# One-hot forms on VectorE in the edge loops of a two-layer graph network, and a fourth row buffer in its attention layer

## Chip, cores and metric

The kernel runs on one core of a Trainium2 chip. The metric is the device time of one execution in microseconds. The kernel before took 15652.3 us, the median of three runs (15645.26 to 15654.0).

## What is computed

A graph has N = 12500 nodes of D = 128 features and E = 400000 edges, sorted by their target `dst`. Two blocks follow each other, each added to the residual stream. The first is a relational graph convolution (RGCN) in two layers over R = 10 edge types; the second is graph attention (GAT) with 4 heads of 32 channels. The reference, cut to what matters:

```python
edge_type = argmax(edge_attr[:, 16:26], axis=1)            # msg[:, 16:-16]

def rgcn(x, w_rel, root, bias):
    seg = dst * R + edge_type
    mean = segment_sum(x[src], seg) / maximum(segment_sum(1, seg), 1)   # per target and type
    return einsum('nrd,rdo->no', mean.reshape(N, R, D), w_rel) + x @ root + bias

h = relu(layernorm(x))
x = x + rgcn(relu(rgcn(h, w_rel1, root1, b1)), w_rel2, root2, b2)

h = relu(layernorm(x))
xl, xr = h @ W_l, h @ W_r                                  # 4 heads x 32
score = einsum('ehc,hc->eh', leaky_relu(xr[dst] + xl[src], 0.2), att)
ex = exp(score - segment_max(score, dst)[dst])
x = x + segment_sum(ex / segment_sum(ex, dst)[dst] * xl[src], dst) + bias
```

## The kernel before

**Tables and rows.** Each layer first makes a table in HBM with all rows that an edge can ask for. `transform` fills `t1_d` with the ten products of a node's features with the ten relation matrices, one row of 128 floats for each node and type. An edge then needs one row of the table, number `src * 10 + type`, and it contributes that row times 1/count to its target. Layer 1's own loop writes the table of layer 2 (`t2_d`) as its results appear, and layer 2's loop writes the table of GAT (`xl_d`, 132 floats a row, and `xr_d`).

**Groups.** The edges are cut into G = 125 groups of 3200, as 128 partitions by J = 25 columns. Since edges are sorted by target, a group touches fewer than 128 consecutive targets. `gather` (L326 to L332) issues 25 indirect DMAs for a group on GpSimd's queue (L329), each of which brings one row to each of the 128 partitions, into a buffer `xs` of the pool; the pools hold three such buffers in all three layers. The same loop therefore runs three times over 125 groups: layer 1, layer 2, GAT.

**Sums on TensorE.** To add rows by target, VectorE makes for each of the 25 columns a one-hot matrix `s` of 128 edges by 128 targets, times the edge's weight, from a row of the numbers 0 to 127 (`iota`, in SBUF), the target column `dst_f` and the weight column `w` (L351). TensorE multiplies it with the gathered rows and accumulates in PSUM over the columns (L353). Six buffers of `s` let VectorE run ahead. `carry` (L356 to L363) adds what the group before left for a shared target.

**Layer 1** (`load`, `weights`, `work`). `load` finds each edge's type on VectorE: the maximum of ten attributes (L384), a compare and a multiply with the constants `rel_m` of -10 to -1 (L386, L387), a minimum (L389), plus 10 (L390), and from it the row numbers `idx` (L391) that the gathers wait for. It then builds one-hots of type (`rh`, L395) and target (`sb`, L397, 3200 elements a partition in bf16) and counts edges by target and type on TensorE (`pcn`, L401). `weights` for the group before adds the counts that a target has in the neighbouring groups (`pcf`, L409 to L416), takes the counts back to the edges with the one-hot `st` (`by_node`, L334 to L340: the targets of a group as a row, loaded onto all partitions as `db`, compared with the partition's own number `pcol`), and takes the reciprocal (L424 to L428). `work`, two groups behind, makes the sums and from them the next table.

**Layer 2** has only the gathers, the sums with the weights that layer 1 left, a normalization (`normed_T`, whose last step is `hn`, L123) and the projections for GAT, split into three bf16 parts (L506 to L514).

**GAT** (`scores`, `rows`). `scores` gathers the group's rows, brings the targets' `xr` to the edges with `st` on TensorE (L564 to L568), applies ReLU on ScalarE (L571), and multiplies with `att` and reduces on VectorE (L572, L574), in seven chunks of up to four columns; then it takes running maxima over each target. `rows` for the group before needs a value from the group after (`after[-1]`), takes exponentials, multiplies rows by them (`xw`, L626), makes one-hots (`s`, L630), and sums on TensorE (L634). `xw` is the last reader of a row buffer.

**The order of the work.** The framework orders each engine's instructions when the program is built: the loops are written group by group, and the built order interleaves neighbouring groups on each engine by its own planned times. An engine then runs its instructions strictly in that order, so one that waits holds what stands behind it. GpSimd has nothing but gathers in these loops; SP's queue carries the plain loads and stores.

Of the kernel before, what the change touches and what calls it, by code (L numbers as in the profile page):

```python
# [9 lines left out]
F32 = mybir.dt.float32  # L10
I32 = mybir.dt.int32
BF16 = mybir.dt.bfloat16
# [14 lines left out]
def kernel(  # L27
# [84 lines left out]
    def normed_T(pool, psum, xt):  # L112

        st = pool.tile([P, nc.vector.BN_STATS_DIM], F32, name="st")
        nc.vector.bn_stats(st, xt)
        mv = pool.tile([P, nc.vector.BN_AGGR_DIM], F32, name="mv")
        nc.vector.bn_aggr(mv, st)
        sd = pool.tile([P, 1], F32, name="sd")
        nc.scalar.activation(sd, mv[:, 1:2], AF.Sqrt, bias=epsc)
        rs = pool.tile([P, 1], F32, name="rs")  # L120
        nc.vector.reciprocal(rs, sd)
        hn = pool.tile([P, D], F32, name="hn")
        nc.vector.tensor_scalar(hn, xt, mv[:, 0:1], rs, op0=OP.subtract, op1=OP.mult)  # L123
        return relu_T(pool, psum, hn)
# [133 lines left out]
    def relation_consts(pool):  # L258
        rel_m = pool.tile([P, J, R], F32, name="rel_m")
        nc.gpsimd.iota(rel_m, pattern=[[0, J], [1, R]], base=-R, channel_multiplier=0,  # L260
                       allow_small_or_imprecise_dtypes=True)
        return rel_m


    def sorted_edges():
# [3 lines left out]
        with tc.tile_pool(name="sd", bufs=1, space=DRAM) as sd, tc.tile_pool(name="sk", bufs=1) as sk:  # L269
# [11 lines left out]
            nc.vector.tensor_copy(iotab, iota)  # L281
            identb = sk.tile([P, P], BF16, name="identb")
# [51 lines left out]
            def by_node(pool, dpool, g):  # L334
# [4 lines left out]
                nc.vector.tensor_scalar(st.rearrange("q j p -> q (j p)"), db, pcol, None, op0=OP.is_equal)  # L339
# [3 lines left out]
            with tc.tile_pool(name="mid", bufs=1) as mid:  # L343
# [3 lines left out]
                def sums(sp, psum, g, xs):  # L347
                    ps = psum.tile([P, D], F32, name="ps")
                    for j in range(J):
                        s = sp.tile([P, P], F32, name="s")  # L350
                        nc.vector.tensor_scalar(s, iota, dst_f[:, g, j:j + 1], w[:, g, j:j + 1],  # L351
# [13 lines left out]
                def layer1():  # L365
                    with tc.tile_pool(name="fk", bufs=1) as kp, tc.tile_pool(name="fx", bufs=3) as xp, \
# [4 lines left out]
                        rel_m = relation_consts(kp)  # L371
                        iotar = kp.tile([P, J, R], F32, name="iotar")
                        nc.vector.tensor_scalar_add(iotar, rel_m, float(R))
# [5 lines left out]
                        def load(g):  # L379
# [26 lines left out]
                        def weights(g, rh, cn, before, after):  # L406

                            pcf = p1.tile([P, R], F32, name="pcf")
# [18 lines left out]
                            nc.vector.tensor_scalar_max(cs, cs, 1.0)  # L427
                            nc.vector.reciprocal(w[:, g, :], cs)  # L428

                        def work(g, xs, before):  # L430
# [5 lines left out]
                            ps = sums(sp, p2, g, xs)  # L436
# [28 lines left out]
                def layer2():  # L465
                    with tc.tile_pool(name="hk", bufs=1) as kp, tc.tile_pool(name="hx", bufs=3) as xp, \
                            tc.tile_pool(name="hs", bufs=6) as sp, tc.tile_pool(name="hc", bufs=4) as cp, \
                            tc.tile_pool(name="hp", bufs=2, space=PSUM) as p2:
                        bob = bcast_row(kp, bias, "bob")
# [18 lines left out]
                        def work(g, xs, before):  # L488
# [3 lines left out]
                            ps = sums(sp, p2, g, xs)  # L492
# [36 lines left out]
            with tc.tile_pool(name="gk", bufs=1) as kp, tc.tile_pool(name="gx", bufs=3) as xp, \  # L529
# [71 lines left out]
                def rows(g, now, after, before):  # L601
# [41 lines left out]
                    nc.vector.tensor_scalar_add(rd, sm[:, :, C:], 1e-16)  # L643
# [431 lines left out]
```

## Time and profile before

The profiled execution took 15668.01 us; the span of its instructions is 15666.2 us.

| Stage (us from the start) | PE busy | VectorE busy | GpSimd busy | TensorE clock granted |
|---|---|---|---|---|
| layer 1, 479 to 5605 | 2194.95 | 1845.23 | 3340.91 | 0.63 |
| layer 2, 5650 to 10159 | 1824.76 | 1174.33 | 2969.91 | 0.57 |
| GAT, 10197 to 15608 | 2975.87 | 2523.45 | 3434.30 | 0.71 |
| whole span | 7415.8 | 5907.1 | 9747.0 | 0.649 |

The stages are told by the gathers: each begins with the first and ends with the last of its 3125. How to read a group's line: source line, engine, operation, what it writes and reads, how many; then busy time, mean time of one in ns, the idle time of the engine just before these instructions, and who ended most of that idle time. "issue" is time that no traced wait explains, and "remote" a wait whose end no traced instruction explains. A timeline's line has the start and the length in us first, and the idle time before it, with its releaser, in brackets at its end. [...]

### The profile page before, as it was taken

To read this page: it belongs to the slowest core of one execution; us is meant where nothing else is said; L and a number is where in the kernel's file an instruction comes from. 1 tells how busy PE (TensorE), PEld (TensorE's weight loads), DVE (VectorE), ACT (ScalarE), POOL (GpSimd) and SP (SyncE) were. 2 spreads that over 40 slices of the span, in tenths; PEclk is the share of its full clock that TensorE was granted. 3 is DMA by queue.
4 is the path that set the end of the run, shared out by engine and by line. 5 is a ranking of instruction groups with operands and counts; after the bars stand their busy time and mean duration, and the time that the engine had idled before them with its cause. 6 is when DMAs were issued, how large, how long until landed. Compare 5 with 4: busy or idle time off the path is not lost.

```text
span 15666.2 us, 128693 instructions
## 1 busy us (share of the span) xinstructions
PE 7415.8 (47%) x39724; PEld 5085.2 (32%) x39724; DVE 5907.1 (38%) x16500; ACT 1459.9 (9%) x4672; POOL 9747.0 (62%) x9384
## 2 busy tenths in 40 slices
PE   7344444444344433444344444445555555555555
PEld 2223333322232322333233333333333433333333
DVE  5333333333333322222222222244444544444444
ACT  2000000000000000000000000011111111111111
POOL 0566666666666656666666666656666666666665
PEclk9666666666666655555555555567766777767777
DMA  6322323323332211111111111122222222222221
GB/s 202 111 92 91 96 92 96 96 90 95 94 96 92 91 59 53 54 54 54 53 54 55 55 54 54 52 68 63 66 62 64 65 62 66 62 66 65 62 64 51
DMA packets 626065, 1164.38 MB, mean 74 GB/s; under 512 B 196480, under 2 KB 398830, under 8 KB 625390
## 3 DMA queue, kind: packets, MB, share of 16 engines
q0 software_dynamic: 300000, 621.40, 14.7%
q1 hardware_dynamic: 279544, 456.64, 8.8%
q10 hardware_dynamic: 45846, 78.02, 1.4%
q8 instruction: 341, 5.59, 0.1%
q14 instruction: 334, 2.74, 0.1%
HBM read 949.89 MB, written 205.49 MB: 74 GB/s over the span
## 4 chain that ended last, share of the span: by engine, by line
another core or an unknown queue 34%; POOL 19%; PE 19%; issue 14%; DVE 9%; DMA 4%; ACT 1%; ACTq 0%; SPq 0%; DVEq 0%; POOLq 0%
POOL xs L329 19%; PE ps L353 9%; DVE s L351 4%; PE pz L564 2%; PE pt L445 2%; DMA xs<-xl_d,src_i 2%; PE po L634 2%; DVE xw L626 1%; PE pz L568 1%; PE ps L150 1%; DMA xs<-t_d,idx 1%; DMA xt<-in_x_dram 1%; DVE sb L397 1%; PE ptr L128 1%
## 5 line engine op out<-in xcount | busy, mean ns | idle before, releaser
L329 POOL DMA_INDIRECT xs<-t_d,idx x6250 | 6310.8, 1010 | 3815.1 <-issue 2597.7
L353 PE MATMUL ps<-xs,s 128*128 128x128 f32 x12500 | 3119.0, 392 | 4870.9 <-issue 2743.4
L329 POOL DMA_INDIRECT xs<-xl_d,src_i x3125 | 3434.3, 1099 | 2014.9 <-DVE xw L626 1046.8
L353 PEld LDWEIGHTS ps<-xs,s 128*128 128x128 f32 x12500 | 2411.9, 267 | 5713.7 <-issue 3732.0
L351 DVE TENSOR_SCALAR s<-iota,dst_f,w 128x128 f32<-128x128 f32 x6250 | 2019.8, 359 | 5559.5 <-remote 3662.8
L564 PE MATMUL pz<-xs,ident 128*128 128x512 f32 x1750 | 1297.5, 834 | 2097.2 <-DMA xs<-xl_d,src_i 1219.8
L564 PEld LDWEIGHTS pz<-xs,ident 128*128 128x128 f32 x1750 | 355.6, 254 | 2229.6 <-issue 1559.7
L568 PEld LDWEIGHTS <-st 128*128 128x128 bf16 x9375 | 840.9, 126 | 622.7 <-issue 558.1
L572 DVE TENSOR_TENSOR lr<-lr,att 128x512 f32<-128x512 f32 x875 | 533.5, 624 | 1259.3 <-ACT lr L571 855.0
L568 PE MATMUL pz<-xr,st 128*128 128x128 bf16 x9375 | 956.5, 269 | 65.2 <-DVE st L339 49.9
L634 PE MATMUL po<-xw,s 128*128 128x132 f32 x6250 | 848.8, 297 | 76.5 <-DVE xw L626 41.2
L634 PEld LDWEIGHTS po<-xw,s 128*128 128x128 f32 x6250 | 815.9, 208 | 122.6 <-issue 64.4
L362 ACT COPY sm<-ps 128x128 f32<-128x128 f32 x250 | 66.3, 265 | 7564.5 <-PE ps L359 4030.8
L571 ACT ACTIVATE lr<-pz 128x512 f32<-128x512 f32 x875 | 476.8, 551 | 2776.4 <-remote 1425.1
L630 DVE TENSOR_TENSOR s<-iotab,dst_b 128x640 f32<-128x640 bf16 x625 | 506.6, 814 | 420.8 <-PE po L634 354.9
L626 DVE TENSOR_TENSOR xw<-xs,xw 128x640 f32<-128x640 f32 x625 | 484.0, 819 | 156.0 <-ACT xw L625 122.3
L574 DVE TENSOR_REDUCE sc<-lr 128x16 f32<-128x512 f32 x875 | 531.3, 620 | 1.0
L445 PE MATMUL pt<-wall,hT 128*128 128x512 f32 x750 | 504.3, 827 | 57.0 <-ACT hT L130 41.0
L397 DVE TENSOR_TENSOR sb<-iotab,dst_b 128x3200 bf16<-128x3200 bf16 x125 | 434.9, 3479 | 0.9 <-PE pcn L401 0.9
L424 DVE TENSOR_TENSOR cw<-pc,rh 128x250 f32<-128x250 f32 x125 | 51.9, 415 | 726.7 <-remote 619.8
L150 PE MATMUL ps<-wall,hT 128*128 128x512 f32 (+1 forms) x588 | 300.9, 647 | 29.1 <-DVE ts L155 21.4
L445 PEld LDWEIGHTS pt<-wall,hT 128*128 128x128 f32 x750 | 183.4, 268 | 305.1 <-issue 175.8
(187 smaller groups left out, 4532.6 us busy)
## 6 DMA issues: line engine op xcount, KB each, us to landing
db<-drow_d SPq DMA_DIRECT2D x250, 800.0 KB
xs<-t_d,idx POOLq DMA_INDIRECT x6250
t_d<-ts SPq DMA_DIRECT2D x125, 640.0 KB
m<-in_edge_attr_dram SPq DMA_DIRECT2D x125, 525.0 KB
t_d<-ts ACTq DMA_DIRECT2D x98, 640.0 KB
xs<-xl_d,src_i POOLq DMA_INDIRECT x3125
ac<-acc_d SPq DMA_DIRECT2D x250, 64.0 KB
xr_d<-xp SPq DMA_DIRECT2D x125, 96.0 KB
```

The source lines that it names most:

```text
L329: nc.gpsimd.indirect_dma_start(out=xs[:, j, :], out_offset=None, in_=table, in_offset=bass.IndirectOffsetOnAxis(ap=ids[:, j:j + 1], axis=0))
L351: nc.vector.tensor_scalar(s, iota, dst_f[:, g, j:j + 1], w[:, g, j:j + 1], op0=OP.is_equal, op1=OP.mult)
L353: nc.tensor.matmul(ps, s, xs[:, j, :], start=(j == 0), stop=(j == J - 1), skip_group_check=True)
L397: nc.vector.tensor_tensor(sb, iotab[:, None, :].to_broadcast([P, J, P]), dst_b[:, g, :, None].to_broadcast([P, J, P]), op=OP.is_equal)
L445: nc.tensor.matmul(pt[:, :n], hT, wall[:, c:c + n], start=True, stop=True)
L564: nc.tensor.matmul(pz[:, :n, :], ident, xs[:, j0:j0 + n, :D], start=True, stop=False, skip_group_check=True)
L568: nc.tensor.matmul(pz[:, j, :], st[:, j0 + j, :], xr[:, k, :], start=False, stop=(k == 2), skip_group_check=True)
L572: nc.vector.tensor_mul(lr[:, :n, :], lr[:, :n, :], att8[:, None, :].to_broadcast([P, n, P]))
L574: nc.vector.tensor_reduce(sc[:, :, j0:j0 + n].rearrange("p h j -> p j h"), lr[:, :n, :].rearrange("p j (h c) -> p j h c", h=H), AX.X, OP.add)
L626: nc.vector.tensor_mul(xw[:, :, :, :C], xs[:, j0:j0 + JW, :D].rearrange("p j (h c) -> p j h c", h=H), xw[:, :, :, C:].to_broadcast([P, JW, ...
L630: nc.vector.tensor_tensor(s, iotab[:, None, :].to_broadcast([P, JW, P]), dst_b[:, g, j0:j0 + JW, None].to_broadcast([P, JW, P]), op=OP.is_ ...
L634: nc.tensor.matmul(po, s[:, j, :], xw[:, j].rearrange("p h a -> p (h a)"), start=(j0 + j == 0), stop=(j0 + j == J - 1), skip_group_check=True)
```

## The change

In the edge loops, instructions of VectorE are written in other forms, and one pool gets a buffer more:

- The row of numbers is copied once in each of layers 1 and 2 to a PSUM tile `iotap`, and the 25 one-hots of a group (`sums`) read it from there.
- `st` (`by_node`, in layer 1 and GAT) is a comparison of two tensors, the second the bf16 column `pcolb` repeated along the row, where it was a comparison with a scalar column. `er` likewise.
- `hn` reads the reciprocal as a repeated tensor, in a form with three operands.
- In layer 1 the type is found as the minimum of `not_equal * 10 + number`, which needs no constants `rel_m` and no addition afterwards; `max(count, 1)` before the reciprocal is dropped, since an edge's own count is at least 1. The PSUM tile `pcf` takes the name `pcn`, and so shares the single buffer of the tile of that name[...].
- GAT's denominators are read from the PSUM tile `po`, not from its copy `sm`.
- GAT's pool of row buffers (`gx`) has four in place of three.

```diff
-        nc.vector.tensor_scalar(hn, xt, mv[:, 0:1], rs, op0=OP.subtract, op1=OP.mult)
+        nc.vector.scalar_tensor_tensor(hn, xt, mv[:, 0:1], rs.to_broadcast([P, D]), op0=OP.subtract, op1=OP.mult)
...
+            pcolb = sk.tile([P, 1], BF16, name="pcolb")
+            nc.vector.tensor_copy(pcolb, pcol)
...
-                nc.vector.tensor_scalar(st.rearrange("q j p -> q (j p)"), db, pcol, None, op0=OP.is_equal)
+                nc.vector.tensor_tensor(st.rearrange("q j p -> q (j p)"), db,
+                                        pcolb.to_broadcast([P, J * P]), op=OP.is_equal)
...
+                def row_in_psum(psum):
+                    t = psum.tile([P, P], F32, name="iotap")
+                    nc.vector.tensor_copy(t, iota)
+                    return t
...
-                        nc.vector.tensor_scalar(s, iota, dst_f[:, g, j:j + 1], w[:, g, j:j + 1],
+                        nc.vector.tensor_scalar(s, iotap, dst_f[:, g, j:j + 1], w[:, g, j:j + 1],
                                                 op0=OP.is_equal, op1=OP.mult)
...
-                        rel_m = relation_consts(kp)
+                        iotap = row_in_psum(p1)
                         iotar = kp.tile([P, J, R], F32, name="iotar")
-                        nc.vector.tensor_scalar_add(iotar, rel_m, float(R))
+                        nc.gpsimd.iota(iotar, pattern=[[0, J], [1, R]], base=0, channel_multiplier=0,
+                                       allow_small_or_imprecise_dtypes=True)
...
-                            eq = wp.tile([P, J, R], F32, name="eq")
-                            nc.vector.tensor_tensor(eq, z, mx[:, :, None].to_broadcast([P, J, R]), op=OP.is_equal)
-                            nc.vector.tensor_mul(eq, eq, rel_m)
+                            lt = wp.tile([P, J, R], F32, name="lt")
+                            nc.vector.tensor_tensor(lt, z, mx[:, :, None].to_broadcast([P, J, R]), op=OP.not_equal)
+                            nc.vector.scalar_tensor_tensor(lt, lt, float(R), iotar, op0=OP.mult, op1=OP.add)
                             rel = wp.tile([P, J], F32, name="rel")
-                            nc.vector.tensor_reduce(rel, eq, AX.X, OP.min)
-                            nc.vector.tensor_scalar_add(rel, rel, float(R))
+                            nc.vector.tensor_reduce(rel, lt, AX.X, OP.min)
...
-                            pcf = p1.tile([P, R], F32, name="pcf")
+                            pcf = p1.tile([P, R], F32, name="pcn")
...
-                                nc.vector.tensor_scalar(er, iota[0:1, :], eb[0:1, g:g + 1], None, op0=OP.is_equal)
+                                nc.vector.tensor_tensor(er, iota[0:1, :], eb[0:1, g:g + 1].to_broadcast([1, P]),
+                                                        op=OP.is_equal)
...
-                            nc.vector.tensor_scalar_max(cs, cs, 1.0)
...
+                        iotap = row_in_psum(p1)
                         bob = bcast_row(kp, bias, "bob")
...
-            with tc.tile_pool(name="gk", bufs=1) as kp, tc.tile_pool(name="gx", bufs=3) as xp, \
+            with tc.tile_pool(name="gk", bufs=1) as kp, tc.tile_pool(name="gx", bufs=4) as xp, \
...
-                    nc.vector.tensor_scalar_add(rd, sm[:, :, C:], 1e-16)
+                    nc.vector.tensor_scalar_add(rd, po.rearrange("p (h a) -> p h a", h=H)[:, :, C:], 1e-16)
```

More of the change, by code (lines that the diff above doesn't have):

```diff
@@ L256, in analyse @@
             nc.vector.tensor_copy(eb, pb[:, 1, :])
[L258 to L262, printed above, removed]
     def sorted_edges():
@@ L345, in sorted_edges, with sums @@
                 w = mid.tile([P, G, J], F32, name="w")
-                def sums(sp, psum, g, xs):
+                def row_in_psum(psum):
+                    t = psum.tile([P, P], F32, name="iotap")
+                    nc.vector.tensor_copy(t, iota)
+                    return t
+                def sums(sp, psum, iotap, g, xs):
                     ps = psum.tile([P, D], F32, name="ps")
@@ L435, in work @@
                             nc.sync.dma_start(xb, xb_d[ds(b, P), :])
-                            ps = sums(sp, p2, g, xs)
+                            ps = sums(sp, p2, iotap, g, xs)
                             sm = carry(cp, ps, g, before, D)
@@ L467, in layer2 @@
                             tc.tile_pool(name="hs", bufs=6) as sp, tc.tile_pool(name="hc", bufs=4) as cp, \
+                            tc.tile_pool(name="hp1", bufs=1, space=PSUM) as p1, \
                             tc.tile_pool(name="hp", bufs=2, space=PSUM) as p2:
+                        iotap = row_in_psum(p1)
                         bob = bcast_row(kp, bias, "bob")
@@ L491, in work @@
                             nc.sync.dma_start(ac, acc2_d[g])
-                            ps = sums(sp, p2, g, xs)
+                            ps = sums(sp, p2, iotap, g, xs)
                             sm = carry(cp, ps, g, before, D)
```

## The prediction

> **What bounds the kernel now.** I read the page first, for the busy engine and its groups; then the GpSimd groups of each stage alone; then timelines of GpSimd and VectorE in one iteration of layer 2 and of layer 1; then who waits for whom in the GAT stage.
>
> ```profile
> POOL 0566666666666656666666666656666666666665
> ...
> L329 POOL DMA_INDIRECT xs<-t_d,idx x6250 | 6310.8, 1010 | 3815.1 <-issue 2597.7
> ...
> L329 POOL DMA_INDIRECT xs<-xl_d,src_i x3125 | 3434.3, 1099 | 2014.9 <-DVE xw L626 1046.8
> ...
> L351 DVE TENSOR_SCALAR s<-iota,dst_f,w 128x128 f32<-128x128 f32 x6250 | 2019.8, 359 | 5559.5 <-remote 3662.8
> ```
>
> GpSimd does nothing but row gathers and is the busiest engine from the first edge group to the last. VectorE's one-hots (L351) stand behind 5559 us of idle time, most of it "remote": no traced instruction ended the wait.
>
> The groups of GpSimd in layer 1 (479 to 5605 us), layer 2 (5650 to 10159) and GAT (10197 to 15608):
>
> ```profile
> L329 POOL DMA_INDIRECT xs<-t_d,idx x3125 | 3340.9, 1069 | 2231.4 <-issue 1709.1 <-DVE idx L391 447.0 <-PE ps L353 29.3
> ...
> L329 POOL DMA_INDIRECT xs<-t_d,idx x3125 | 2969.9, 950 | 1583.7 <-issue 888.6 <-PE ps L353 320.5 <-remote 267.7
> ...
> L329 POOL DMA_INDIRECT xs<-xl_d,src_i x3125 | 3434.3, 1099 | 2014.9 <-DVE xw L626 1046.8 <-issue 908.7 <-DVE rest L512 39.1
> ```
>
> Busy plus idle is 5572, 4554 and 5449 us. The pace at which gathers follow each other undisturbed is in the timelines below: 0.945 us and 0.30 us of issue. For 3125 gathers that is 2953 + 938 = 3891 us, in each stage. The rest splits in two. Busy time over 2953 is gathers held up: 388, 17 and 481 us. Idle time over 938, less each stage's first wait (447, 46, 39 us), is GpSimd waiting for a buffer or an index: 846, 600 and 1038 us. These 2484 us of gaps and 886 us of hold-ups are what a change can win.
>
> Layer 2, GpSimd and then VectorE:
>
> ```profile
> 7532.03 0.94 POOL L329 DMA_INDIRECT xs<-t_d,idx  x1 [0.30 <-issue]
> 7533.27 0.97 POOL L329 DMA_INDIRECT xs<-t_d,idx  x1 [0.30 <-issue]
> 7539.16 0.97 POOL L329 DMA_INDIRECT xs<-t_d,idx  x1 [4.91 <-PE ps L359]
> ...
> 7501.80 1.88 DVE L351 TENSOR_SCALAR s<-iota,dst_f,w 128x128 f32<-128x128 f32 x7 [1.06 <-PE ps L353]
> ...
> 7524.65 0.35 DVE L351 TENSOR_SCALAR s<-iota,dst_f,w 128x128 f32<-128x128 f32 x1 [3.21 <-remote]
> 7528.19 0.35 DVE L351 TENSOR_SCALAR s<-iota,dst_f,w 128x128 f32<-128x128 f32 x1 [3.19 <-issue]
> 7533.08 0.35 DVE L351 TENSOR_SCALAR s<-iota,dst_f,w 128x128 f32<-128x128 f32 x1 [4.54 <-remote]
> 7537.29 0.35 DVE L351 TENSOR_SCALAR s<-iota,dst_f,w 128x128 f32<-128x128 f32 x1 [3.86 <-remote]
> 7538.71 1.63 DVE L351 TENSOR_SCALAR s<-iota,dst_f,w 128x128 f32<-128x128 f32 x6 [1.07 <-PE ps L353]
> ```
>
> While gathers run, one-hots come 3.5 to 4.9 us apart; in GpSimd's pause (7534.2 to 7539.2) they come 0.27 us apart. Rows landed long before, so data isn't missing. The loop feeds on itself: gathers starve the one-hots of an older group, that group keeps its buffer, and GpSimd pauses about 5 us in every group until VectorE has caught up.
>
> Layer 1 shows the opposite hold: VectorE on GpSimd.
>
> ```profile
> 2895.21 3.48 DVE L397 TENSOR_TENSOR sb<-iotab,dst_b 128x3200 bf16<-128x3200 bf16 x1
> 2895.60 3.91 POOL L329 DMA_INDIRECT xs<-t_d,idx  x1 [0.30 <-issue]
> 2899.81 0.94 POOL L329 DMA_INDIRECT xs<-t_d,idx  x1 [0.30 <-issue]
> ```
>
> One gather takes 3.91 us because it meets the 3.48 us one-hot sb, a two-input form: 2.96 us lost. Layer 1's whole hold-up, 388 us over 125 groups, is 3.1 us a group. Where within its 1.25 us a gather meets sb varies, so the loss does too; counting each lengthened gather to the VectorE instruction that overlaps it most, 2.7 us a group are sb's, the rest L339's and L351's. In GAT:
>
> ```profile
> POOL xs L329 <- DVE xw L626: 1046.8, 97, 40.8
> ...
> PE pz L564 <- DMA xs<-xl_d,src_i: 1219.8, 362, 19.4
> ```
>
> GpSimd waits for the release of a row buffer by xw, while TensorE waits for rows: neither is saturated, and three buffers tie them together.
>
> [...] L424, PSUM input, 250 elements, 415 ns against 412 for L386 from SBUF[...]. [...] sb, so built, takes 3479 ns for 3200 elements (1.04 ns each and some 150)[...].
>
> **The change part by part.**
>
> *The one-hots of layers 1 and 2 (6250 of L351) read PSUM.* Price of one: 415 ns less 122 x 1.04 = 288 ns, 359 now. [...] nothing should stop them during gathers. TensorE then sets their pace: where nothing held them, twelve matmuls (six edge columns of two passes) took 2.93 us on TensorE's timeline, so 25 columns take 12.2 us. A group's work of 12 to 15 us fits under 31 us of gathers, with two buffers' slack. Layer 2's 600 us of gaps go; I leave 10. Its two-input forms (L495, L497, L512 twice, now L123) take 0.29 us each and cost little: the present hold-up is 17 us, and I keep 10. Layer 2: 46 + 3891 + 10 + 10 = 3957, against 4554: -597. In layer 1 the next index chain (L384 to L391) stands on VectorE behind these one-hots, so its gaps have the same source. In the built order the chain still follows the older group's one-hots; without waits VectorE needs about 25 x 0.5 us, 7 us for sb and st, and some 5 us on TensorE, 25 us in all, before the next index is ready. I leave 40 us of 846.
>
> *st (L339), 250 times, becomes two-input.* Now 1064 ns; then as sb, 3479 ns. On VectorE that adds 2.4 us a group, which lies beside gathers: VectorE is busy 1845 of 5126 us in layer 1 and 2523 of 5411 in GAT. On GpSimd it doesn't hide: as sb it should hold gathers 2.7 us a group. Bounds: what st costs already (by the same count 0.2 us a group in layer 1 and 1.1 in GAT, 134 us), and 3.4, its whole length. I take 2.7, 340 us a stage.
>
> Layer 1: 447 + 3891 + sb 340 + st 340 + others 25 + gaps 40 = 5083, against 5572: -489.
>
> *The fourth row buffer in GAT.* Gather group g+3 must now wait for xw of group g; in the built order that stands behind up to four score chunks of group g+2, hence pauses of 12 us after a group ends. With four buffers the waiting group is g+4: one whole group's gathers, 37 us, lie between. The gaps go if compute keeps up. TensorE waits for rows 1220/125 = 9.8 us of its 43.4 us a group, so it needs about 33.6, and st's 2.4 makes 36; GpSimd needs 31.1 and hold-ups. These are now 481 us, of them 134 by the present st; the other 347 arise while GpSimd works, 80% of the time, so 434 when it always does; with 340 of st, 774 us, or 37.3 us a group in all. The two are close: I leave 100 us of gaps. GAT: 39 + 3891 + 774 + 100 = 4804, against 5449: -645. The whole gain here hangs on compute needing under 37 us.
>
> *One answer each, zero:* the dropped add and max of layer 1 (0.18 and 0.23 us) and the merged PSUM tile (pcf waits for the scalar copy of pcn, under 0.5 us twice a group; TensorE is busy 2195 of 5126 us): slack of the gathers covers them, and without it they would cost at most 125 us. hn in three-operand form, about 0.29 for 0.35 us, beside gathers; in the first 390 us it is 98 times -0.06. The denominators from PSUM; the iota on GpSimd ahead of the first index; pcolb and row copies, once.
>
> **Sum.** -597 - 489 - 645 = -1731 us. The profiled execution took 15668.0 (its span 15666.2 and 1.8 around it), 15.7 above the median 15652.3. 15668 - 1731 = 13937, less 16: about 13920.
>
> **Rivals.**
> - *GAT is bound by compute.* For it: 36 against 37 us is close, and the order interleaves two groups with ScalarE waits (pz for lr, 514 us). Against it: TensorE waits for rows a fifth of the time. At 41.5 us a group GAT ends 3 us x 125 = 390 higher: 14310.
> - *Two-input holds are cheaper than sb's.* If st costs what it does now and gaps vanish: 315 + 206 + 150 lower, 13250; at half of that, 13580. For it: some st fall into pauses or next to sb; against: gathers never pause then.
> - *The new one-hot still contends, and st's hold comes on top (slower).* For it: the two scalar columns still come from SBUF, and no row shows such a form. Then layers 1 and 2 keep their gaps, and st adds 2.4 us to VectorE's catch-up in a pause plus 2.5 to a run in layer 1 (613 us). GAT gains nothing if its chain, lengthened by st's 2.4 us, is the bound (300 us). 15652 + 913 is 16570. It decides when gaps shrink by less than 2.5 us a group. Against: two-input forms start within gathers freely.
>
> **How the numbers follow.** Forecast 0.64, compute-bound GAT 0.18, cheap holds 0.12, slower 0.06. Range 13550 to 14450: cheap holds at half, up to compute-bound GAT with 140 us of gaps left in layer 1. A difference under 0.2% can't be told from none here. Faster 0.93, same 0.01, slower 0.06.
>
> **What would show it.** One-hots in layer 2 about 0.5 us apart during gathers, their "remote" idle gone; GpSimd's idle in layer 2 near 1000 us; gathers of 3 to 4 us beside st in layer 1 and GAT, their busy time near 3660 and 3730 us; no wait for xw over 1 us in most GAT groups. Wrong if one-hots still come 3 us apart, if st doesn't lengthen a gather, or if GpSimd still waits for xw.

## The result, and the profile after

The kernel after takes 17071.66 us (median of 4 runs, 17048.29 to 17082.26) where the kernel before, on the same chip, takes 15648.78 (4 runs, 15638.42 to 15654.0): 1.0908 times as long, 95% interval 1.0889 to 1.0927. The profiled execution's span is 17060.9 us. The page of the kernel after; its lines stand a few further down: gathers L325, one-hots L354, st L335, sb L400, cw L428.

```profile
POOL 0454444444444444666666666666677677766665
...
L325 POOL DMA_INDIRECT xs<-t_d,idx x6250 | 5928.8, 949 | 5413.9 <-issue 4109.3
...
L325 POOL DMA_INDIRECT xs<-xl_d,src_i x3125 | 3862.1, 1236 | 1737.8 <-issue 933.7
...
L354 DVE TENSOR_SCALAR s<-iotap,dst_f,w 128x128 f32<-128x128 f32 x6250 | 2262.6, 401 | 5072.2 <-remote 3579.7
```

In layers 1 and 2 the gathers themselves became shorter (5928.8 us for 6310.8), but GpSimd's idle time grew from 3815.1 to 5413.9. One one-hot takes 401 ns, not less than 359, and still stands behind 5072 us of idle time, "remote" as before. The groups of GpSimd in layer 1 (479 to 6704 us), layer 2 (6748 to 11375) and GAT (11419 to 16975):

```profile
L325 POOL DMA_INDIRECT xs<-t_d,idx x3125 | 2971.2, 951 | 3699.6 <-issue 3206.6 <-DVE idx L394 446.7 <-PE ps L356 38.9
...
L325 POOL DMA_INDIRECT xs<-t_d,idx x3125 | 2957.5, 946 | 1714.2 <-issue 902.7 <-PE ps L356 743.9 <-PE ptr L486 45.2
...
L325 POOL DMA_INDIRECT xs<-xl_d,src_i x3125 | 3862.1, 1236 | 1737.8 <-issue 933.7 <-DVE xw L631 756.1 <-ACT xr L319 44.3
```

Counted from the gathers' starts and ends in the two traces, means per group of 25 gathers in us ("hold-up" is what gathers last over 0.945 us each; the run contains it):

| Stage | before: run, hold-up, pause, period | after: run, hold-up, pause, period | whole stage, before to after, us |
|---|---|---|---|
| layer 1 | 34.06, 3.14, 7.00, 41.08 | 31.11, 0.16, 18.83, 49.94 | 5125 to 6224 |
| layer 2 | 31.08, 0.17, 5.02, 36.10 | 30.98, 0.05, 6.08, 37.06 | 4507 to 4627 |
| GAT | 34.79, 3.88, 8.56, 43.38 | 38.21, 7.28, 6.28, 44.55 | 5410 to 5556 |

So the stages changed by +1099, +119 and +146 us, where the forecast had -489, -597 and -645. The loss lies in layer 1: its pauses grew by 11.83 us a group, while its hold-ups shrank by 2.98. A timeline of layer 1 after, in order of time:

```profile
2502.45 0.78 PE L404 MATMUL pcn<-rh,sb 128*128 128x10 bf16 x25
2502.80 0.95 POOL L325 DMA_INDIRECT xs<-t_d,idx  x1 [19.14 <-issue]
...
2504.95 0.17 ACT L406 CAST cn<-pcn 128x10 bf16<-128x10 f32 x1 [3.93 <-remote]
...
2506.07 0.85 PE L426 MATMUL pc<-cf,st 128*128 128x10 bf16 x25
...
2521.42 0.42 DVE L428 TENSOR_TENSOR cw<-pc,rh 128x250 f32<-128x250 f32 x1 [17.42 <-remote]
...
2532.80 0.94 POOL L325 DMA_INDIRECT xs<-t_d,idx  x1 [0.30 <-issue]
...
2538.31 4.27 DVE L354 TENSOR_SCALAR s<-iotap,dst_f,w 128x128 f32<-128x128 f32 x13 [2.42 <-remote]
2542.82 3.48 DVE L400 TENSOR_TENSOR sb<-iotab,dst_b 128x3200 bf16<-128x3200 bf16 x1
2547.28 3.47 DVE L335 TENSOR_TENSOR st<-db,pcolb 128x3200 bf16<-128x3200 bf16 x1
2552.42 0.95 POOL L325 DMA_INDIRECT xs<-t_d,idx  x1 [18.67 <-issue]
```

Two things are to be seen. cw (the counts of each edge, the step before its weight) needs only pc and rh; rh was done at 2502.4 and TensorE ended pc at 2506.9, yet cw starts at 2521.4, and the group's last 19 one-hots stand behind it on VectorE. And in GpSimd's pause (2533.7 to 2552.4) thirteen one-hots, sb and st stand one after the other ahead of the next idx: 4.6 us of waiting, 4.3 of one-hots, 3.5 and 3.5, and 2.9 of small steps. In the kernel before, the sb that stood behind idx was the next group's, and in 111 of 125 groups it started while a gather ran.

In layer 2 after, the one-hots from PSUM come as far apart as those from SBUF did:

```profile
9030.98 0.94 POOL L325 DMA_INDIRECT xs<-t_d,idx  x1 [0.30 <-issue]
9031.42 0.41 DVE L354 TENSOR_SCALAR s<-iotap,dst_f,w 128x128 f32<-128x128 f32 x1 [3.10 <-remote]
...
9034.98 0.41 DVE L354 TENSOR_SCALAR s<-iotap,dst_f,w 128x128 f32<-128x128 f32 x1 [3.15 <-remote]
...
9039.22 0.41 DVE L354 TENSOR_SCALAR s<-iotap,dst_f,w 128x128 f32<-128x128 f32 x1 [3.83 <-remote]
```

That speaks against the forecast of one-hots about 0.5 us apart. What ends these waits is in the trace's semaphore events, its records of the engines' signals to each other: a one-hot waits for TensorE's signal that the matmul six columns earlier has read its buffer. Of layer 2's one-hots with over 1 us of idle before them, 84% (before) and 90% (after) start within 60 ns of a TensorE signal, the median 26 ns after it. The other direction is prompt, as in the kernel before, where TensorE follows each one-hot here within 0.06 us:

```profile
7524.65 0.35 DVE L351 TENSOR_SCALAR s<-iota,dst_f,w 128x128 f32<-128x128 f32 x1 [3.21 <-remote]
7525.05 0.79 PE L353 MATMUL ps<-xs,s 128*128 128x128 f32 x2 [2.76 <-DVE s L351]
...
7528.19 0.35 DVE L351 TENSOR_SCALAR s<-iota,dst_f,w 128x128 f32<-128x128 f32 x1 [3.19 <-issue]
7528.60 0.79 PE L353 MATMUL ps<-xs,s 128*128 128x128 f32 x2 [2.75 <-issue]
```

Counted over layer 2 of before, from the fourth gather of a run on: the 877 matmuls with over 0.5 us of idle before them start a median 0.06 us after their one-hot's end, while the 982 one-hots with over 1 us of idle start a median 7.9 us after the end, a modelled one, of the matmul six columns earlier. VectorE was ready; TensorE's signal was late.

### The profile page after: what moved, and what is told of

Its sections match the earlier page's. It is cut to its first block, busy times and chain, and to the rows that moved or that the text cites. A ratio compares the mean times of both kernels' runs of the same rounds, so it can differ in the third digit from the quotient of the medians.

```text
span 17060.9 us, 129013 instructions
## 1 busy us (share of the span) xinstructions
PE 7289.5 (43%) x39724; PEld 5124.2 (30%) x39724; DVE 6728.8 (39%) x16252; ACT 1464.2 (9%) x4672; POOL 9792.8 (57%) x9384
## 4 chain that ended last, share of the span: by engine, by line
another core or an unknown queue 43%; DVE 16%; POOL 14%; PE 12%; issue 12%; DMA 3%; ACT 1%; ACTq 0%; SPq 0%; DVEq 0%; POOLq 0%
POOL xs L325 14%; DVE s L354 8%; PE ps L356 5%; PE pt L448 2%; DVE sb L400 2%; PE pz L569 1%; DMA xs<-t_d,idx 1%; PE po L639 1%; PE ps L150 1%; DVE st L335 1%; DMA xs<-xl_d,src_i 1%; DVE xw L631 1%; PE pz L573 1%; DMA xt<-in_x_dram 1%
## 5 line engine op out<-in xcount | busy, mean ns | idle before, releaser
L325 POOL DMA_INDIRECT xs<-t_d,idx x6250 | 5928.8, 949 | 5413.9 <-issue 4109.3
L356 PE MATMUL ps<-xs,s 128*128 128x128 f32 x12500 | 3275.1, 413 | 6095.1 <-DVE s L354 3104.3
L325 POOL DMA_INDIRECT xs<-xl_d,src_i x3125 | 3862.1, 1236 | 1737.8 <-issue 933.7
L356 PEld LDWEIGHTS ps<-xs,s 128*128 128x128 f32 x12500 | 2571.1, 287 | 6810.7 <-DVE s L354 3497.9
L354 DVE TENSOR_SCALAR s<-iotap,dst_f,w 128x128 f32<-128x128 f32 x6250 | 2262.6, 401 | 5072.2 <-remote 3579.7
L569 PE MATMUL pz<-xs,ident 128*128 128x512 f32 x1750 | 1091.4, 715 | 1891.2 <-issue 821.0
L639 PE MATMUL po<-xw,s 128*128 128x132 f32 x6250 | 913.5, 304 | 346.1 <-issue 231.5
L573 PE MATMUL pz<-xr,st 128*128 128x128 bf16 x9375 | 864.2, 252 | 261.3 <-DVE st L335 203.3
L573 PEld LDWEIGHTS <-st 128*128 128x128 bf16 x9375 | 744.6, 116 | 659.1 <-issue 434.4
L428 DVE TENSOR_TENSOR cw<-pc,rh 128x250 f32<-128x250 f32 x125 | 52.4, 419 | 2118.9 <-remote 2016.2
L335 DVE TENSOR_TENSOR st<-db,pcolb 128x3200 bf16<-128x3200 bf16 x250 | 868.9, 3476 | 38.2 <-PE pz L573 29.9
L400 DVE TENSOR_TENSOR sb<-iotab,dst_b 128x3200 bf16<-128x3200 bf16 x125 | 435.1, 3481 | 0.6 <-PE pcn L404 0.6
```

The lines of the kernel that those rows point to most:

```text
L325: nc.gpsimd.indirect_dma_start(out=xs[:, j, :], out_offset=None, in_=table, in_offset=bass.IndirectOffsetOnAxis(ap=ids[:, j:j + 1], axis=0))
L335: nc.vector.tensor_tensor(st.rearrange("q j p -> q (j p)"), db, pcolb.to_broadcast([P, J * P]), op=OP.is_equal)
L354: nc.vector.tensor_scalar(s, iotap, dst_f[:, g, j:j + 1], w[:, g, j:j + 1], op0=OP.is_equal, op1=OP.mult)
L356: nc.tensor.matmul(ps, s, xs[:, j, :], start=(j == 0), stop=(j == J - 1), skip_group_check=True)
L400: nc.vector.tensor_tensor(sb, iotab[:, None, :].to_broadcast([P, J, P]), dst_b[:, g, :, None].to_broadcast([P, J, P]), op=OP.is_equal)
L569: nc.tensor.matmul(pz[:, :n, :], ident, xs[:, j0:j0 + n, :D], start=True, stop=False, skip_group_check=True)
```

## The experiments

My theory after the result: while GpSimd issues gathers, TensorE's signals reach the other engines seldom and late; in a pause they come in a burst; so whatever hangs on them advances in pauses, and the order on VectorE decides what a pause contains. The rivals: the one-hots' source in SBUF (as predicted), the long st, the relation lines by themselves, late rows, too many signals. A group of runs shares a chip with the kernel before; times are only compared within a group.

**e1: the kernel after with layer 1's old relation lines** (the edit in short notation).

```diff
-lt = (z != mx); lt = lt * R + iotar; rel = min(lt)
+eq = (z == mx); eq = eq * rel_m; rel = min(eq); rel = rel + R
+cs = max(cs, 1.0)
```

> The kernel after, but with layer 1's edge types worked out as in the kernel before (eq, its product with rel_m, minimum, plus 10, and the clamp of cs). Order theory: in the kernel after, shortening this chain let the planner put the one-hot sb (3.5 us) and 17 columns' one-hots ahead of idx, so that all of it runs while GpSimd waits for its indices; with the old lines the built order has sb behind idx again, the gap per group in layer 1 falls from 18.8 us to about 9 to 11, the gathers are held some 3 us per group by sb again, and the time is 16000 to 16500 us. Rival, the PSUM one-hots and the long st themselves: the gap stays at 16 to 19 us and the time above 16900.

15510.04 us against 15499.31: ratio 0.9998 (0.9982 to 1.0013). Layer 1 has 38.91 us a group: run 36.45, hold-up 5.52, pause 2.41. This one edit undoes the whole loss, more than I had expected, though st and the PSUM one-hots are still in. In the built order an sb is behind idx again, the next group's: a group's pcn reads an sb that ended a median 35 us earlier (41 in the kernel before, 7 in the kernel after). The timeline of e1:

```profile
2510.93 3.47 DVE L409 TENSOR_TENSOR sb<-iotab,dst_b 128x3200 bf16<-128x3200 bf16 x1
2511.46 3.76 POOL L332 DMA_INDIRECT xs<-t_d,idx  x1 [0.30 <-issue]
...
2512.38 0.77 PE L413 MATMUL pcn<-rh,sb 128*128 128x10 bf16 x25
...
2513.19 0.17 ACT L415 CAST cn<-pcn 128x10 bf16<-128x10 f32 x1 [0.24 <-PE pcn L413]
...
2514.39 0.77 PE L435 MATMUL pc<-cf,st 128*128 128x10 bf16 x25
...
2515.52 0.94 POOL L332 DMA_INDIRECT xs<-t_d,idx  x1 [0.30 <-issue]
2516.08 0.42 DVE L437 TENSOR_TENSOR cw<-pc,rh 128x250 f32<-128x250 f32 x1 [1.49 <-PE ps L363]
```

sb holds GpSimd inside one gather, pcn, cn and pc are done meanwhile, and cw follows 0.9 us after pc. The hold that the prediction counted as a cost is also a window for signals. That is not this group alone: pcn ends inside a held gather in 110 of e1's 125 groups and 111 of before's, and ScalarE's cn starts a median 0.04 us after it in both. In the kernel after pcn ends in an unheld first gather in 118 groups, and cn starts 1.70 us after it. From pc's end to cw it is a median 1.5 us in e1, 1.7 in before and 14.4 in after.

**e2: the kernel before with PSUM one-hots in layer 2 alone.**

```diff
+iotap = row_in_psum(p1)      # layer 2
-nc.vector.tensor_scalar(s, iota, dst_f[..], w[..], ...)
+nc.vector.tensor_scalar(s, iotap, dst_f[..], w[..], ...)
```

> The kernel before, with only layer 2's one-hots reading the index row from PSUM. Prediction's theory [...]: layer 2's gaps go, about 15050 us. Theory of late TensorE signals (each one-hot waits for the matmul six columns back, whose signal comes 2 to 5 us late while gathers run): one-hots stay 2 to 5 us apart, layer 2 is 0 to 1 us per group longer, 15640 to 15780 us.

15512.05 us against 15499.31, ratio 1.0002 (0.9992 to 1.0011); layer 2 takes 4451 us, and 4445 and 4446 with SBUF one-hots in e3 and e4 on the same chip. The PSUM source frees nothing.

**e3: the kernel before with the two-input st alone.**

```diff
-nc.vector.tensor_scalar(st.., db, pcol, None, op0=OP.is_equal)
+nc.vector.tensor_tensor(st.., db, pcolb.to_broadcast([P, J * P]), op=OP.is_equal)
```

> The kernel before, with only the transposed one-hot st of layer 1 and of the GAT stage in the two-input form. If it is only longer (3.48 us in place of 1.06) and lies ahead of idx in layer 1: layer 1 grows by 2.4 us a group, 300 us, and the GAT stage by 2.5 to 3.5 us of hold-up a group, 300 to 440 us: 16250 to 16400 us. If it frees the gathers as meant: below 15650. If layer 1's gap reaches 18.8 us as in the kernel after: layer 1 alone would add 1100 us, above 16700.

15978.55 us, ratio 1.0302 (1.0269 to 1.0335), less than expected. GAT grows to 5892 us (5327 in e2, whose GAT is that of before; hold-up 7.40 for 4.03 us a group), but layer 1 shrinks from 5107 to 5040: its hold-up rises by 1.70 us and its pause falls by 2.24.

**e4: the kernel before with the fourth row buffer alone** (`name="gx", bufs=4`).

> The kernel before, with only the fourth row buffer in the GAT stage. If GpSimd there waits for a buffer that comes free late: the gaps of 8.6 us fall to about 5 with the hold-up of 3.9 us a group unchanged, GAT about 440 us shorter, 15200 us. If the stage is bound by VectorE's and TensorE's own chain: GAT stays at 5410 us, 15600 to 15680 us in all. The prediction had the gaps gone but for single waits: 14900 to 15050.

15507.77 us against 15499.31, ratio 1.0000 (0.9986 to 1.0014): GAT 5370 us, against 5327 in e2. Pauses over 0.35 us are 61 and not 98, but their sum is 1078 us against 949: fewer and longer. Beside the long st the buffer seems worth more: 5892 us in e3 (three buffers), 5515 in e1 (four, and the denominators from PSUM).

**e5: the kernel after, sb tied behind rel.**

```diff
+dg = rel * 0 + dst_b[:, g, :]
-sb = (iotab == dst_b[:, g, :])
+sb = (iotab == dg)
```

> The kernel after with every edit kept, but sb's comparison in layer 1 reads dg, a copy of the group's dst_b that a small added instruction makes from rel (times zero) and dst_b; so sb can't be put ahead of rel, and in the built order it stands behind idx. If the place of sb and of the columns ahead of idx is the cause: layer 1 at 38.5 to 40.5 us a group as with the old relation lines, 15450 to 15750 us. If it was the relation lines' own forms or counts: the gap stays near 19 us, above 16700.

16733.77 against 15650.17, ratio 1.0706 (1.0677 to 1.0734): the expectation failed. Layer 1 goes from 49.94 to 47.57 us a group only (hold-up 3.26, pause 13.38). This place of sb is worth 2.4 us of the 11. What is left shows in what VectorE's cw waited for, in the kernel after, in e5 and in e1:

```profile
DVE cw L428 <- remote: 2016.2, 113, 49.5
```
```profile
DVE cw L430 <- remote: 1122.4, 120, 16.0
```
```profile
DVE cw L437 <- PE ps L363: 260.8, 91, 3.7
DVE cw L437 <- remote: 148.5, 13, 39.4
```

16, 9 and 3 us a group. But e5 is not e1's order: tied to rel, sb is its own group's, and pcn has to wait for it (it starts a median 0.06 us after sb's end). So the chain from pcn over cn, cf and pc to cw begins when the hold is over, where in e1 it runs inside it. In the group whose gathers start at 2504.0 us the hold ends at 2508.3, pc ends at 2511.0 between running gathers, and cw starts at 2517.1; over all groups cn is a median 0.89 us and cw 6.2 us late. So e5 does not price sb's old place.

**e6: the kernel before with 26 buffers for s** in layers 1 and 2 (`bufs=26` for `bufs=6`).

> The kernel before, with 26 buffers for s in layers 1 and 2 in place of 6, so that no one-hot waits for a matmul of its own group. If late signals from TensorE pace the one-hots: they run 0.3 to 0.4 us apart while gathers run, layer 2's gaps fall from 4.6 us to about 0.3 (layer 2 3900 to 4000 us), layer 1's too by some us, 14500 to 14950 us. If the one-hots are starved [...] (the prediction's theory): still 2 to 5 us apart, 15450 to 15600 us.

16358.19 us, ratio 1.0452 (1.0434 to 1.0469). Neither expectation came out. Layer 2 hardly moves: 35.74 us a group with a pause of 4.71, where before had 36.10 and 5.02. Of its one-hots with over 1 us of idle, 85% still start within 60 ns of a TensorE signal, so 26 buffers didn't free them of it. Layer 1 got slower as in the kernel after, though its relation lines are the old ones: in its built order too sb stands ahead of idx (pcn follows its sb after 3.7 us). Its hold-up is 0.24, its pause 15.98, and cw waits 3977 us in all.

**e7: layer 2's sums read a fixed tile; the gathers run, nobody reads them.** The output is not the reference's from layer 2 on.

> The kernel before, but layer 2's sums read a fixed tile of zeros; the gathers still run into their buffers, which nobody reads. So layer 2's result and all after it are not the reference's. If TensorE's signals come late because gathers run at all: the one-hots stay 2 to 5 us apart during gathers, and layer 2 still takes 4300 us or more. If they come late because each matmul waits for a gather's own semaphore: the one-hots run 0.3 to 0.5 us apart, and layer 2 falls to the gathers' own 3900 us.

16342.66 us, ratio 1.0441 (1.0420 to 1.0462). No matmul waits for a row, no gather for a matmul. The gathers of layer 2 end at 10057.9 us, but GAT's first starts only at 10891, because the sums lag so far behind. VectorE in e7, first beside gathers, then after the last:

```profile
8414.26 0.35 DVE L351 TENSOR_SCALAR s<-iota,dst_f,w 128x128 f32<-128x128 f32 x1 [5.03 <-issue]
8419.86 0.35 DVE L351 TENSOR_SCALAR s<-iota,dst_f,w 128x128 f32<-128x128 f32 x1 [5.25 <-issue]
8425.46 0.35 DVE L351 TENSOR_SCALAR s<-iota,dst_f,w 128x128 f32<-128x128 f32 x1 [5.25 <-issue]
```
```profile
10093.60 0.29 DVE L495 TENSOR_TENSOR x<-sm,ac 128x128 f32<-128x128 f32 x1 [0.17 <-ACT sm L362]
...
10101.92 0.29 DVE L495 TENSOR_TENSOR x<-sm,ac 128x128 f32<-128x128 f32 x1 [0.16 <-ACT sm L362]
```

Beside gathers one one-hot in 5.60 us, in step with every fourth gather; without them a whole group of 25 in 8.32 us. So it isn't the rows, the row buffers or the matmuls' own waits: it is that gathers run, as the first of the two expectations had it.

**e8, e9, e10: fewer signals; e1 with fewer signals; e7 with a quarter of the bytes.**

```diff
 # e8, layer 2: tiles of five one-hots, last column first
-for j in range(J): s = tile(P, P); s <- ...; matmul(ps, s, xs[:, j, :])
+for j0 in range(J - 5, -1, -5):
+    s = tile(P, 5, P); five s[:, j, :] <- ...
+    for j in range(4, -1, -1): matmul(ps, s[:, j, :], xs[:, j0 + j, :])
 # e10
-gather(xp, t2_d[:N * R, :], idx[:, g, :], D)
+gather(xp, t2_d[:N * R, :].rearrange("n (a c) -> (n a) c", a=4), idx[:, g, :], 32)
```

> The kernel before, with layer 2's sums done in tiles of five one-hots, the columns taken from the last to the first: the one-hots, their number and form are as before, but TensorE now has to signal 9 times a group for them and not 25. If the rate at which TensorE's signals come through while gathers run is the limit (some 13 a group were seen to come in a run of 25 gathers): layer 2's gaps fall from 4.6 to 5.0 us to under 1 us, layer 2 3900 to 4050 us, ratio to before 0.965 to 0.977. If VectorE itself is starved (the prediction's theory) or the rows are late: layer 2 stays at 4440 to 4510 us, ratio 0.998 to 1.002.

> The kernel after with the old relation lines (as in e1) and layer 2's sums with 9 signals a group (as in e8). The two parts lie in different stages: layer 1 at 38.9 us a group, layer 2 near the gathers' own 31.2 us, GAT as after; ratio to before 0.962 to 0.977. If signals are not the limit in layer 2: 0.998 to 1.002, as e1.

> As e7 (layer 2's sums read a fixed tile of zeros, nobody reads what is gathered, the results from there on are not the reference's), but each gathered row has 32 numbers and not 128, so a quarter of the bytes. If the rows' bytes hold the signals back: TensorE's signals come through in far greater number than e7's 3.9 a group, and from layer 2's first gather to GAT's takes 3900 to 4300 us. If it is the issuing of the gathers or their count: as e7, about 5200 us, one signal in 5 to 7 us.

This group lay on another chip, and there the kernel before takes 13814.12 us (23 runs). The ratios, 1.0003 (0.9994 to 1.0012), 1.0081 (1.0064 to 1.0098) and 0.9991 (0.9982 to 1.0001), say nothing of the question, but the traces do. Layer 1 of e8 and e10 is that of the kernel before, with one-hots from SBUF: 34.6 us a group, no pause over 0.35 us. The copy sm starts 0.04 us after its matmul in every group, in layers 1 and 2, and in the second half of a run of gathers about one TensorE signal comes per gather. On this chip the signals aren't late.

**f1 to f4: the kernel after, e8, e9 and e10 once more,** on a chip where the kernel before takes 15648.83 us (26 runs).

> The kernel after once more, unchanged, beside the others of this group. Where the kernel before takes 15500 us or more: ratio 1.08 to 1.10, layer 1 at 49 to 51 us a group. Where the kernel before takes about 13800 us (TensorE's signals about one per gather): no pause is needed for them, so layer 1 at about 34 to 38 us a group, ratio 0.98 to 1.02, as e9 had.

> As e8 (the kernel before with 9 signals a group in place of 25 for layer 2's sums). Where the kernel before takes 15500 us or more: if the rate of TensorE's signals is the limit, layer 2's gaps fall from 4.6 to 5.0 us to under 1 us, ratio 0.965 to 0.977; if VectorE is starved or rows are late, 0.998 to 1.002. Where it takes about 13800: 0.999 to 1.001, as e8.

> As e9 (the kernel after with the old relation lines and layer 2's sums with 9 signals a group). Where the kernel before takes 15500 us or more: ratio 0.962 to 0.977 if signals are the limit, 0.998 to 1.002 if not. Where it takes about 13800: 1.006 to 1.010, as e9.

> As e10: layer 2's sums read a fixed tile of zeros, nobody reads what is gathered, rows have 32 numbers in place of 128; results from layer 2 on are not the reference's. Where the kernel before takes 15500 us or more: if the rows' bytes hold the signals back, from layer 2's first gather to GAT's 3900 to 4300 us; if it is the issuing or the count of gathers, about 5200 us and some 4 signals a group, as e7. Where it takes about 13800: 3930 us, as e10.

f1: ratio 1.0897 (1.0872 to 1.0922), layer 1 at 49.96 us a group, as in the first comparison. f4: 1.0444 (1.0423 to 1.0465), as e7: bytes are not the cause. f3: 1.0014 (1.0000 to 1.0028); its layer 1 differs from f1's in the relation lines alone and takes 4971 us where f1's takes 6226 on the same chip. f2: 0.9993 (0.9986 to 1.0001), layer 2 with a pause of 4.60 us a group: the number of signals is not the limit either, and that part of my second theory fell. By its ratio f2 would also fit late rows or a VectorE kept from working; the timeline of its layer 2 shows other engines waiting, for a matmul that is done:

```profile
8410.74 0.58 PE L372 MATMUL ps<-sm,ecol 128*1 128x128 f32 x2
...
8424.16 0.94 POOL L329 DMA_INDIRECT xs<-t_d,idx  x1 [0.30 <-issue]
...
8429.55 0.27 ACT L375 COPY sm<-ps 128x128 f32<-128x128 f32 x1 [27.76 <-remote]
8429.74 0.94 POOL L329 DMA_INDIRECT xs<-t_d,idx  x1 [4.64 <-remote]
```

All of a group's matmuls were done at 8411.3. The copy that waits for the last one starts 18.2 us later, 4.45 us after the last gather's end, and GpSimd, which had stopped because it too waited for TensorE (for the row buffer), goes on 0.2 us after it. Over 122 groups of f2 the lag from the matmul's end, which is a modelled one, to the copy has a median of 17.5 us (e6: 25.2; before: 6.5), and the copy comes a median 4.39 us after the last gather (e6: 4.47; before: 4.58). The first burst of TensorE signals (three within 1 us) comes 4.1 to 4.4 us after the last gather in layer 2 of before, after, e1, e4 and f2 alike (medians). The last packet of the group's rows has ended 1.2 us after that gather (before and f2), so the burst does not wait for rows. A pause that ends on such a signal, as the release of a row buffer is one, lasts about that long or longer here.

**g1 to g4.** g1: f2 with ten s tiles and five row buffers in layer 2. g2: e1 with st and the three row buffers of before in GAT; the denominators stay those of the kernel after. g3: both. g4: e7 with a GpSimd fill of a 128x512 tile after each gather of layer 2.

> As f2 (the kernel before with layer 2's sums in tiles of five, last column first), and ten such tiles in place of three and five row buffers in place of three in layer 2: no one-hot and no gather then waits for a signal of its own group. Where the kernel before takes 15500 us or more: if GpSimd pauses only because the release of its row buffer is signalled late, and the rest of the group (three signals in a chain) fits into a run of gathers, layer 2's gaps fall from 4.6 us to under 1 us, layer 2 3900 to 4050 us, ratio 0.965 to 0.977. If the chain of a group gets its signals only in a pause, every group still needs one: gaps of 4.5 us a group on average, 0.998 to 1.002. Where the kernel before takes about 13800: 0.998 to 1.002.

> e1 (the kernel after with the old relation lines), but the GAT stage as in the kernel before: st in the one-input form there, three row buffers. Where the kernel before takes 15500 us or more: layer 1 gains 180 to 250 us as in e1 and f3, layer 2 and GAT as before, ratio 0.984 to 0.990. Where it takes about 13800: layer 1 at 37.1 us a group against 34.6, 300 us longer, ratio 1.020 to 1.024.

> g2 with layer 2 of g1. Where the kernel before takes 15500 us or more: 0.948 to 0.966 if g1's gaps go, as g2 if they don't.

> As e7 (layer 2's sums read a fixed tile of zeros, nobody reads what is gathered, results from there on are not the reference's), but in layer 2 GpSimd fills a scratch tile of 128x512 after each gather, so that gathers don't stand back to back. Where the kernel before takes 15500 us or more: if TensorE's signals are held by gathers following one another at 1.25 us, they come at once here (some tenths of a us), each group's work takes under 12 us and layer 2 ends with its gathers; if any gathering at all holds them, the lags stay at several us and layer 2's work ends some 800 us behind the gathers, as in e7. Where it takes about 13800: no lag in either case.

Again a chip with prompt signals (before 13821.83 us, 23 runs): 0.9998 (0.9991 to 1.0004), 1.0158 (1.0141 to 1.0175), 1.0165 (1.0148 to 1.0182), and 15080.01 for g4, a single run without an interval. They tell nothing of late signals. g2 and g3 were expected at 1.020 to 1.024 on such a chip; layer 1 lost what was expected (4634 us in g2, 4321 in g1), but GAT took 4940 us in both, against 5006 to 5023 with the stage of before (g1, g4, e8, e10). The denominators from PSUM are the only edit of that stage in g2, so they seem worth some 70 us there, about which the prediction had said zero. The same two instructions as above, in g1:

```profile
6014.12 0.38 PE L372 MATMUL ps<-sm,ecol 128*1 128x128 f32 x2
6014.54 0.27 ACT L375 COPY sm<-ps 128x128 f32<-128x128 f32 x1 [24.41 <-PE ps L372]
```

Here the copy starts 0.04 us after the matmul's end, amid running gathers.

## Why the prediction was wrong

**The step that failed** is that, with the row in PSUM, "nothing should stop them during gathers." The row in SBUF had not stopped them. e2 gives them the PSUM source and layer 2 takes 4451 us for 4445 and 4446; on the chips of e8 and g1 the SBUF one-hots of layer 1 run beside gathers of the same pace without a pause (34.6 us a group in e8, 4321 us for the 125 groups in g1); and where they wait in layer 2 of before, a TensorE signal ends the wait, a median 7.9 us after the matmul. That gathers stop a one-hot because of its source was my reading of "remote" idle beside gathers; no trace had shown it. That a two-input form holds gathers is seen again (GAT's hold-up 3.88 to 7.28 us).

**The gaps, -489, -597 and -645 us.** The first two rest on that step, the third on the fourth buffer. Layer 2 kept its gaps. I priced its one-hot at 288 ns, an estimate: 122 columns at the 1.04 ns of sb's, taken off the 415 ns of L424's 250. It takes 401, 42 more than before. That is not what made the +119 us: e1's layer 2 has the same instructions in the same order as that of the kernel after and takes 4447 us, against 4445 and 4446 with the old forms on its chip (e3, e4). In the kernel after and f1, on chips where the kernel before is slower, it took 4627 and 4631; why is open.

**The order in layer 1.** "In the built order the chain still follows the older group's one-hots" was true and was read too lightly: the built order also had sb moved ahead of idx, and I left 40 us of gaps. The "zero" for the shorter relation lines, "at most 125 us", was the dearest item of the list: on one chip they make layer 1 1255 us longer (f1 and f3). With them sb moved ahead of idx, so sb and st fell into the pause, and cw's chain fell out of sb's hold into running gathers, cw 14.4 us behind pc. That the lines cost this is shown (e1, f3), and e6, with the old lines, has sb ahead of idx too and a like loss (layer 1 5877 us). That cw's lag does it is read from the lags of all groups and was not tried by itself, since e5 put sb into a third place.

**st.** 340 us a stage by holding gathers: GAT's hold-up grew by 3.40 us a group, 425 us. In layer 1 st fell into the pause (hold-up 0.16). Where it did meet gathers in layer 1, on the prompt chip, the hold-up rose by 2.45 us a group (5.82 in e9, 3.37 in e8), near the 2.7 that I took. The short two-input forms met gathers without a wait: in layer 2 of before 116 of 125 L495 start while a gather runs, behind 4.0 us of idle in all.

**The fourth buffer.** "The gaps go if compute keeps up" failed on the late chips: e4 gains nothing, and the kernel after keeps 6.28 us of pause a group. What ends these pauses was not tried. With the long st, e1's GAT is 377 us shorter than e3's, the edit of the denominators included. On a prompt chip the buffer did what was forecast: GAT has 96 pauses over 0.35 us in e8 and 97 in g2, none in e9.

**The rivals.** "Slower", at 16570, had the sign, the gaps that stay and VectorE's catch-up in the pause; its cause, a new one-hot that still contends, is not what ended the waits, and its price for layer 1, 613 us, was too low. I had given it 0.06. The other two don't hold where signals are prompt: e9's GAT has 38.71 us a group and no pause, so compute doesn't bind it at 41.5, and the holds of st are not cheap.

Where signals are prompt, the sum's arithmetic does hold for the new forms: e9, which is the kernel after but for the relation lines and layer 2's tiles, takes 13931.62 us with layer 2 at 3908 and GAT at 4833 (forecast 3957 and 4804, each with its first wait). But there the kernel before has no gaps to win in layers 1 and 2, so that e9's total lies beside the forecast 13920 confirms no gain, and e9 is 0.8% slower than the kernel before: st's holds cost layer 1 305 us (37.07 less 34.61 us a group) and GAT wins 190. The kernel after itself was not run on such a chip.

No version beat both kernels. On chips with late signals e1 ties with before; its layer 1 wins 251 us and its GAT loses 188. g2, which was to keep only the gain, came on a prompt chip, so that stays open.

## What to carry to other kernels

Before an idle stretch is put down to what runs beside it, look at which semaphore ended it: of layer 2's one-hots with over 1 us of idle before them, 84 and 90% started within 60 ns of a TensorE signal, and that was what they waited for. Where one engine issues indirect gathers back to back, count the signals from TensorE that a loop needs per round, and see in the built order which of them fall into a pause or a hold of the gathers; a few VectorE instructions less can move that order and cost more than they save (layer 1 of f1 against f3: 1255 us; from pc to cw 14.4 us in after and 1.5 in e1). And measure on more than one chip before a gap is called the kernel's own.

## What the runs showed of the hardware

- Two kinds of times (each chip was used for one group of runs, so a chip is not told apart from its group). The same kernel before takes 15499, 15650 and 15649 us on three chips (and 15649 on the one of the first comparison, which may be one of them) and 13814 and 13822 on two others, with gathers of 0.945 + 0.30 us on all. What differs is how late TensorE's signals come beside gathers: from the matmul to the copy sm in layer 2 it is a median 6.5 us in before, 17.5 in f2 and 25.2 in e6 on the late chips, and 0.04 us in e8 and g1 on the prompt ones. Why the chips differ is open.
- The records differ likewise. For 9375 gathers, e8 on a prompt chip has 149497 events of the gathers' semaphores, 15.9 a gather; on the late chips before has 35420 and f2 40380, 3.8 and 4.3 a gather. Whether fewer come there or fewer are recorded isn't told apart. A missing event is no late signal: of VectorE's 15719 signals in before 10285 events are on record, and yet TensorE follows its one-hots after 0.06 us.
- In layer 2 of before TensorE's signals become later as a run of gathers goes on. A one-hot that waits starts a median 0.04 us after the matmul six columns earlier where that matmul ended in the run's third or fourth gather, 4.7 us where it ended in the sixth, and 13.3 us where it ended in the eighth. The copy sm follows its matmul after a median 0.04 us where that matmul ended in a run's first gather: in 27 of 125 groups of before, and in 116 of 125 of after, which was on a late chip too. In layer 1 of after the lag is 1.70 us (pcn to cn) in the first gather already. While a gather was held by sb (before, e1) it was 0.04 us.
- A one-hot of 128x128 with its row in PSUM took 401 ns, from SBUF 359. The two-input st took 3476 ns where the one-input form took 1064.
